# Input rows 20 KB apart in memory instead of 16 KB, in a kernel that multiplies pairs of fields

## The chip, the cores and the metric

The kernel runs on one core of one Trainium2 chip. The metric is the device time of one execution in microseconds (us). "Before" and "after" are the two kernels of the change. A run counts as slow when it is over 1.5% above the fastest of the same kernel, and as fast otherwise.

## The reference

```python
# x: (4096, 32, 64) float32, W: (64, 64) float32
vid = jnp.einsum('bfd,de->bfe', x, W)
idx_i, idx_j = jnp.triu_indices(32, k=1)          # 496 pairs of fields, i < j
return x[:, idx_i, :] * vid[:, idx_j, :]          # (4096, 496, 64)
```

The output has 520 MB and the input 33.6 MB, so this is mostly a matter of writing.

## The kernel before

The host lays x out as 16 tiles of 128 rows (two batch halves x 64 embedding elements). A row holds 32 fields of 128 samples, 512 B each, thus 16 KB; rows follow one another without a gap. One row goes to one SBUF partition. A tile is loaded in pieces of eight fields (the second tile in two of sixteen), so a piece is 128 runs of 4 KB, one from each row, and the distance from one run to the next is the row pitch.

```python
C = 128          # samples per row of a tile
SLOT = 83        # pairs per output buffer
# GROWING: sizes of the first 25 stores, so that stores start early and grow  [list cut]

    NT, _, F, _ = x.shape                    # 16 tiles, 32 fields
    xpool = ctx.enter_context(tc.tile_pool(name="x", bufs=2))
    opool = ctx.enter_context(tc.tile_pool(name="out", bufs=4))
    # [psum, const and scheduling cut]

    def load(t, pieces, queue):
        xt = xpool.tile([P, F, C], F32, tag="x", name=f"x_{t}")
        n = F // pieces
        for lo in range(0, F, n):
            queue.dma_start(out=xt[:, lo : lo + n, :], in_=x[t][:, lo : lo + n, :])
        return xt

    loaded = [load(0, 4, nc.sync), load(1, 2, nc.sync)]
    for t in range(NT):
        if 0 < t < NT - 1:
            loaded.append(load(t + 1, 4, nc.scalar))
        # TensorE: vid = W^T x for the tile, 8 PSUM banks            [cut]
        # VectorE: o[pair] = x[i] * vid[j], runs of i for one j      [cut]
        # SyncE: store each filled stretch of the output buffer      [cut]

# host
    x = x.reshape(2, NT, C, F, D).transpose(1, 0, 4, 3, 2).reshape(NT, 2 * D, F, C)
```

Of the kernel before, what the change touches and what calls it, by code (L numbers as in the profile page):

```python
# [1 line left out]

# [4 lines left out]

F32 = mybir.dt.float32
ALU = mybir.AluOpType

P = 128

C = 128

SLOT = 83

GROWING = [
    21, 24, 21, 17, 22, 15, 16, 30, 24, 20, 21, 18, 27, 24, 32, 46, 37, 50,
    31, 45, 38, 53, 30, 65, 18,
]  # L20


def first(j):

    return j * (j - 1) // 2


@with_exitstack
def pairwise_bilinear_kernel(
    ctx: ExitStack,  # L30
    tc: tile.TileContext,
    x: bass.AP,
    w: bass.AP,
    out: bass.AP,
):

    nc = tc.nc
    NT, _, F, _ = x.shape
    D = P // 2
    NP = F * (F - 1) // 2  # L40

    BANK = 512 // C


    ctx.enter_context(tc.manual_schedule(engines={mybir.EngineType.SP}))

    const = ctx.enter_context(tc.tile_pool(name="const", bufs=1))
    xpool = ctx.enter_context(tc.tile_pool(name="x", bufs=2))
    opool = ctx.enter_context(tc.tile_pool(name="out", bufs=4))
    psum = ctx.enter_context(  # L50
        tc.tile_pool(name="ps", bufs=8, space=bass.MemoryType.PSUM)
    )


    w2 = const.tile([P, D], F32)
    nc.sync.dma_start(out=w2, in_=w)  # L56
# [10 lines that stand above are left out]
    done = 0  # L67
    growing = iter(GROWING)
    until = next(growing)
# [3 lines that stand above are left out]
        xt = loaded[t]  # L73


        vid = []
        for b in range(0, F, BANK):
            pv = psum.tile([P, BANK, C], F32, tag="pv", name=f"pv_{t}_{b}")
            for h in range(2):
                half = slice(h * D, (h + 1) * D)  # L80
                nc.tensor.matmul(  # L81
                    pv[half, :, :],
                    lhsT=w2[half, :],
                    rhs=xt[half, b : b + BANK, :],
                    start=True,
                    stop=True,
                )
            vid.append(pv)

        sent = 0  # L90
        for j in range(1, F):
            i = 0
            while i < j:
                at = first(j) + i
                base = at - at % SLOT
                if at == base:
                    ot = opool.tile([P, SLOT, C], F32, tag="o", name=f"o_{t}_{at}")
                n = min(j - i, base + SLOT - at)
                nc.vector.tensor_tensor(  # L99
                    ot[:, at - base : at - base + n, :],  # L100
                    xt[:, i : i + n, :],
                    vid[j // BANK][:, j % BANK : j % BANK + 1, :].to_broadcast([P, n, C]),
                    ALU.mult,
                )
                i += n
                at += n
                if t * NP + at == until or at in (base + SLOT, NP):
                    nc.sync.dma_start(
                        out=out[t][:, sent:at, :],
                        in_=ot[:, sent - base : at - base, :],  # L110
                    )
                    sent = at
                    if t * NP + at == until:
                        until += next(growing, NT * NP)


_INS = ["r_x", "L0_rec_W"]
_OUTS = [((4096, 496, 64), "float32")]


# [32 lines left out]
```

## Time and profile before

| Before, profiled run | |
|---|---|
| median of three runs | 1294.66 us (1294.46 to 1294.67) |
| span in the profile | 1293.3 us |
| bytes moved, mean rate | 553.82 MB, 428 GB/s |
| VectorE busy | 1102.4 us (85%) |
| TensorE busy | 229.0 us (18%) |
| load packets of 4 KB in the steady state | 7168, median 159 ns |

A packet is one piece of a transfer as one DMA engine records it, here the run of one row.

The page cuts the span into 40 slices of 32 us: a digit is the busy share of a slice in tenths, and the row GB/s has what the 16 DMA engines moved in each. In the table of queues, q1 carries what SyncE issued (all stores and the first two tiles' loads) and q10 what ScalarE issued (the other loads), with packets, MB and the share of 16 engines' span. The chain of work that ended last is read backwards from the end; in its order of time each line is start, duration, and work. The lines themselves are in the prediction.

### The profile page before, as it was taken

Reading aid. Unit: us, or ns where it says so; the run is one execution under the profiler, and the core shown is the slowest. Engines: PE = TensorE matmul, PEld = TensorE weight load, DVE = VectorE, ACT = ScalarE, POOL = GpSimd, SP = SyncE. Lnnn points to the kernel's source line nnn. Section 1 sums busy time; section 2 is a strip of 40 time slices with the busy share of each in tenths; the row PEclk is TensorE's granted clock in tenths of the full one; section 3 lists DMA queues with packets and bytes.
Section 4 is the critical chain, followed back from the end, with each engine's and each line's share of the span. In section 5 each row is a group of like instructions: output and inputs, shape, how many; then the busy total and the mean of one; then the engine's idle time right before and its main releaser. Section 6 shows DMA issues by size and latency. Waiting matters only on the chain.

```text
span 1293.3 us, 2181 instructions
## 1 busy us (share of the span) xinstructions
PE 229.0 (18%) x512; PEld 49.5 (4%) x512; DVE 1102.4 (85%) x576; POOL 0.2 (0%) x4
## 2 busy tenths in 40 slices
PE   4121121211212112121121211203112031120000
PEld 1000000000000000000000000000000000000000
DVE  7999999888898888988888888888888888888970
POOL 0000000000000000000000000000000000000000
PEclk8555555555655555565555655556555565555555
DMA  9999999999999999999999999999999999999998
GB/s 376 427 410 434 434 433 434 431 433 431 434 431 433 431 432 433 432 431 435 432 431 433 432 435 426 437 427 433 434 430 435 430 431 436 428 436 431 438 431 348
DMA packets 25212, 553.82 MB, mean 428 GB/s; under 512 B 2928, under 2 KB 2928, under 8 KB 10736
## 3 DMA queue, kind: packets, MB, share of 16 engines
q1 hardware_dynamic: 17136, 524.33, 94.2%
q10 hardware_dynamic: 8064, 29.36, 5.6%
q8 instruction: 4, 0.07, 0.0%
q14 instruction: 8, 0.07, 0.0%
HBM read 33.59 MB, written 520.09 MB: 428 GB/s over the span
## 4 chain that ended last, share of the span: by engine, by line
DMA 66%; DVE 29%; issue 1%; DVEq 0%; PE 0%; SPq 0%
DMA out_dram<-o 65%; DVE o L99 29%; DMA x<-in_r_x_dram 0%; DVEq L145 0%; PE pv L81 0%; DVEq L99 0%; SPq L56 0%
## 5 line engine op out<-in xcount | busy, mean ns | idle before, releaser
L99 DVE TENSOR_TENSOR o<-x,pv 128x640 f32<-128x640 f32 (+14 forms) x576 | 1102.4, 1984 | 151.3 <-DMA out_dram<-o 142.2
L81 PE MATMUL pv<-x,w 64*64 64x512 f32 x512 | 229.0, 1027 | 951.7 <-DVE o L99 500.2
L81 PEld LDWEIGHTS pv<-x,w 64*64 64x64 f32 x512 | 49.5, 205 | 1129.5 <-issue 1124.8
L128 POOL MEMSET const-bfloat16-1.0<- 128x1 bf16 x1 | 0.1, 102 | 0.0
L128 POOL MEMSET const-uint8-127<- 128x1 uint8 x1 | 0.1, 102 | 0.0
L128 POOL MEMSET const-float32-0.0<- 128x1 f32 x1 | 0.1, 99 | 0.2 <-issue 0.2
L128 POOL MEMSET const-float32-1.0<- 128x1 f32 x1 | 0.1, 99 | 0.0
## 6 DMA issues: line engine op xcount, KB each, us to landing
out_dram<-o SPq DMA_DIRECT2D x72, 5312.0 KB, 41.4
out_dram<-o SPq DMA_DIRECT2D x15, 5184.0 KB, 42.3
x<-in_r_x_dram ACTq DMA_DIRECT2D x56, 512.0 KB, 31.9
out_dram<-o SPq DMA_DIRECT2D x3, 1536.0 KB, 8.3
out_dram<-o SPq DMA_DIRECT2D x1, 4160.0 KB, 23.5
out_dram<-o SPq DMA_DIRECT2D x3, 1344.0 KB, 6.4
out_dram<-o SPq DMA_DIRECT2D x2, 1920.0 KB, 15.3
out_dram<-o SPq DMA_DIRECT2D x1, 3392.0 KB, 22.2
```

What stands on the lines that cost most here:

```text
L81: nc.tensor.matmul(pv[half, :, :], lhsT=w2[half, :], rhs=xt[half, b : b + BANK, :], start=True, stop=True,)
L99: nc.vector.tensor_tensor(ot[:, at - base : at - base + n, :], xt[:, i : i + n, :], vid[j // BANK][:, j % BANK : j % BANK + 1, :].to_broad ...
L128: nc = _bacc.Bacc("TRN2", target_bir_lowering=False, num_devices=1, dynamic_dma_scratch_size=1024)
```

## The change

The change pads each row of x with eight unused fields, so that rows start 20 KB apart, which is not a power of two. Its hope is that reads from evenly spaced rows spread better over the memory. The pad is never loaded.

```diff
 SLOT = 83
+
+PAD = 8
...
-    NT, _, F, _ = x.shape
+    NT = x.shape[0]
+    F = x.shape[2] - PAD
...
     x = x.reshape(2, NT, C, F, D).transpose(1, 0, 4, 3, 2).reshape(NT, 2 * D, F, C)
+    x = _np.pad(x, ((0, 0), (0, 0), (0, PAD), (0, 0)))
```

## The prediction

> **What bounds the kernel now.** I read the page's table of busy time first, then its slices and queue table, then the chain of work that ended last, then the waits, and last the single packets of the two data queues.
>
> ```profile
> DVE  7999999888898888988888888888888888888970
> DMA  9999999999999999999999999999999999999998
> GB/s 376 427 410 434 434 433 434 431 433 431 434 431 433 431 432 433 432 431 435 432 431 433 432 435 426 437 427 433 434 430 435 430 431 436 428 436 431 438 431 348
> q1 hardware_dynamic: 17136, 524.33, 94.2%
> q10 hardware_dynamic: 8064, 29.36, 5.6%
> HBM read 33.59 MB, written 520.09 MB: 428 GB/s over the span
> DMA 66%; DVE 29%; issue 1%; DVEq 0%; PE 0%; SPq 0%
> ```
>
> The reader should see three things. The 16 DMA engines are at nine tenths or more in 39 of 40 slices, and from the fourth slice on they move 426 to 438 GB/s with no trend. The two queues together fill 94.2 + 5.6 = 99.8% of 16 engines' span, so there is no idle DMA time to speak of. And the traffic is lopsided: 520 MB are written, 34 MB read. VectorE is busy 1102.4 us of 1293.3 (85%), so it has 15% to spare.
>
> The chain in order of time shows how the bound works. Four output buffers circulate: VectorE refills one, its store queues behind three others, and when it lands the next refill may begin.
>
> ```profile
> 604.73 11.09 DVE o L99 x3
> ...
> 615.84 42.24 DMA out_dram<-o
> ...
> 658.17 11.49 DVE o L99 x5
> ```
>
> One lap is 11.1 + 42.2 = 53.3 us, four stores. A batch tile has six stores and one load, (496 + 32) x 64 KB = 34.6 MB; four sixths of it is 23.1 MB, and 23.1 MB in 53.3 us is 433 GB/s. So the lap is not a latency that some cleverness could shorten; it is the time in which the DMA engines move one lap's bytes. A store alone would need 5.44 MB / 433 GB/s = 12.6 us, and takes 41.4 us to land since it stands behind its predecessors.
>
> Last, the waits. They say whether a late load could hurt by its lateness alone.
>
> ```profile
> PE pv L81 <- DMA x<-in_r_x_dram: 432.0, 36, 16.9
> DVE o L99 <- DMA out_dram<-o: 142.2, 78, 3.2
> DVE o L99 <- PE pv L81: 9.1, 2, 8.4
> ```
>
> TensorE waits for the loads of x, but it is only 18% busy and runs ahead. VectorE waits for TensorE twice in the whole program, at the very start (8.4 us and the rest), and otherwise only for stores that free a buffer. Loads are therefore early enough; what they cost is the engine time that they take from the stores.
>
> **What the Trainium skill says.** The page "DMA: Bandwidth & Descriptors", section "Latency and other measured facts", is the one that bears on the change: with copies of 128 partitions it found 207 GB/s per direction at a row pitch of 512 KiB, 164 at 2 MiB, 103 at 4 MiB, and the full 214 when 4 KiB were added to the last. Its cause, channels hit in lock-step, it calls an inference. So padding does help where the pitch is a large power of two; but at 512 KiB the loss was already down to 3%, and here the pitch is 16 KiB, thirty-two times smaller. Whether this trace agrees is tested on the packets below. The same page, section "Where 436 GB/s comes from", gives a ceiling of 435.2 GB/s for one core's 16 engines. The trace agrees: a plateau of 433. The same page, section "Issuing engines are not separate DMA queues", says that transfers of all issuers share the same engines; q1 and q10 adding to 99.8% agree with it. So a microsecond of engine time saved or lost on loads is one saved or lost in the end.
>
> **The change part by part.** The code that runs is the same. Comparing the two builds, every engine has as many instructions in the same order (VectorE 576 multiplications, 62 loads of x, 112 stores); only line numbers move. The number of fields is taken from the padded shape less eight, so the pad is never loaded. Load pieces are still 4 KB per partition (two of them 8 KB, in the first two tiles' ramp), on-chip tiles keep their size, and the output's layout is untouched. Removed: nothing. Added on the device: nothing. Moved: the address at which each partition's row of x starts, 20 KB apart instead of 16, and with it, perhaps, where the allocator puts the tensors in memory, as x grows from 33.6 to 41.9 MB.
>
> So the only thing that can change is the time of a read packet. From the trace's packet records, leaving out those of a few bytes (mean of the loads, medians, ns):
>
> ```
> load  in the steady state   4096 B  x7168   median 159 (10th and 90th percentile both 159), mean 160.2
> load  at the start          4096 B  x512    median 159, 90th percentile 324, mean 200.4
> load  at the start          8192 B  x256 and stores of that size: median 309
> store                      42496 B  x9216   median 1571, mean 1573.0
> ```
>
> From the first and last row: (1571 - 159) / (42496 - 4096) = 0.03677 ns per byte, which is 27.2 GB/s for one engine and 435 for sixteen; the rest, 159 - 4096 x 0.03677 = 8.4 ns, is the same for a packet of 42 KB as for one of 4 KB. The 8 KB row lies on the same line: 8.4 + 301.2 = 309.6, measured 309. Reads at 16 KB pitch and writes at 248 KB pitch thus follow one law, and the reads scatter less than a nanosecond between the percentiles. A channel conflict would show as a longer or spread read packet; there is none to remove. That is my answer to whether the trace agrees with the skill: it does, in that at this small pitch nothing is lost.
>
> Sum of what the change can return:
> - Steady loads: 7168 packets x (159 - 159) = 0 us expected.
> - Scatter of the steady loads: 7168 x (160.2 - 159) / 16 engines = 0.5 us at the very most.
> - The start: 512 x (200.4 - 159) / 16 = 1.3 us of extra packet time. The 8 KB loads directly after it, at the same 16 KB pitch, run at the full rate, so I put this down to the start of an idle memory path and expect no more than a few tenths of it to change.
> - VectorE 1102.4 us, TensorE 229.0 us, stores 94.2%: no change.
>
> Expected: 1294.66 less about 0.2, say 1294.4 us.
>
> **The rivals.** *First: the 16 KB pitch does cost, and padding pays.* For it: it is a power of two, each 4 KB piece visits the same quarter of every 16 KB, and the mean rate of the load packets, 4096 / 160.2 = 25.6 GB/s per engine, is lower than the stores' 27.0. Against it: the 8.4 ns per packet explain that difference wholly. If even these vanished, 7168 x 8.4 / 16 = 3.8 us, plus the 1.3 us of the start, would give 1289.6 us, 0.4% faster. That is the ceiling of this rival; 2% (25.9 us) is out of reach, as all loads together hold only 71.8 us of the engines' time.
>
> *Second: the new pitch or the new places are worse.* Each 10% on a load packet is 7.2 us, and it would reach the end in full, as the DMA engines are the bound. To lose 2% a load packet would have to take 25.9 x 16 / 7168 = 58 ns more, 217 instead of 159. Against it: 20 KB is five times 4 KB and so less regular than 16, still a multiple of every alignment that the old rows had. The stores could be touched too if the output moved to other addresses: 0.2% on them is 2.4 us. That I hold possible and small; their rows of 248 KB pitch stay as they are.
>
> *Third: loads land later or earlier and shift buffers.* A piece takes 31.9 us to land because it shares engines with store packets ten times its size. A shift of a few us there is hidden: VectorE waits for no load after the start, and the order of store bytes does not alter their sum.
>
> **Range and chances.** The three runs of before lie within 0.2 us and the profiled one at 1295.1, so noise on one chip is under half a microsecond. I allow 3 us down (most of the first rival) and 3.5 us up (5% on load packets, or 0.2% on stores with a new place, or another chip): 1291.5 to 1298. Within 2%: 0.975. Faster by over 2% would need more than the loads can give: 0.01. Slower by over 2% needs 36% on each load packet, or a change to the stores that I do not see: 0.015.
>
> **What would show it.** In the profile after: q10 again 8064 packets, 29.36 MB and 5.6%; the steady load packet again 159 ns; q1 at 94.2%; a plateau of 433 GB/s and the lap of 53.3 us; VectorE at 1102 us. If padding pays, q10's share falls towards 5.3% and the load packet towards 151 ns; if it hurts, that share and the spread of its packets grow. A different mean at the start only, beside the same 159 ns later, would show that a pitch matters when reads run alone. The prediction is wrong if store packets change from 1571 ns, since that means that placement matters, which I counted as nearly nothing, or if packet counts change, since then the transfers were cut differently than the code suggests.

## The result

After: 1295.14 us median (1293.85 to 1296.49, four runs); before in the same rounds: 1294.66 us (1294.46 to 1295.46, four runs). The ratio is 1.0003, with a 95% interval of 0.9985 to 1.002. A ratio here is the mean time of one kernel's fast runs over that of the other's in the same rounds, so it is not quite the ratio of the quoted medians. Two later measurements of the same pair gave 1.0002 and 0.9983. The change is worth nothing that matters.

The page of the profile after, in the lines that answer to those of before:

```profile
DVE  7999999888887888888888888888888888888970
DMA  9999999999999999999999999999999999999997
GB/s 388 427 413 438 432 432 432 437 428 433 436 432 432 432 429 430 430 431 435 429 432 430 430 433 432 436 428 430 436 432 437 423 430 440 433 431 429 431 439 323
q1 hardware_dynamic: 17136, 524.33, 94.1%
q10 hardware_dynamic: 8064, 29.36, 5.6%
HBM read 33.59 MB, written 520.09 MB: 428 GB/s over the span
DMA 66%; DVE 29%; issue 2%; DVEq 0%; PE 0%; SPq 0%
```

Packets and bytes are equal to the last digit, the loads' share is 5.6% as before, and the plateau has not moved. The slices between differ by up to 8 GB/s either way; the first rose from 376 to 388 GB/s, the last fell from 348 to 323. Both are taken up below.

The lap of output buffers in the chain of after, at the place shown of before, and the waits:

```profile
605.73 11.10 DVE o L105 x3
...
616.84 42.33 DMA out_dram<-o
...
659.26 11.49 DVE o L105 x5
```

```profile
PE pv L87 <- DMA x<-in_r_x_dram: 429.9, 35, 17.0
DVE o L105 <- DMA out_dram<-o: 144.4, 79, 3.8
DVE o L105 <- PE pv L87: 8.2, 2, 7.5
```

One lap takes 53.4 us instead of 53.3. VectorE still waits for nothing but freed buffers after the start. Its first wait for TensorE, though, is 0.9 us shorter (8.2 instead of 9.1 in total). That is the one sign in these views that could be the new pitch's, and it sits at the start. The chain shows where it comes from, first of before, then of after (start, us, what):

```profile
1.17 5.12 DMA x<-in_r_x_dram
```

```profile
1.17 4.22 DMA x<-in_r_x_dram
```

The first load of 512 KB lands 0.9 us sooner. In stretches of 2 us the table of busy times by window shows the same; the last two columns are the DMA share and GB/s. Before, then after:

```profile
2.00:4.00 2.00, 0.00 (x0) 0.00 (x0) 0.00 (x0) 0.00 (x0) 1.00 0.82 184
4.00:6.00 2.00, 0.00 (x0) 0.00 (x0) 0.00 (x0) 0.00 (x0) 1.00 0.94 309
6.00:8.00 2.00, 1.58 (x4) 0.59 (x6) 0.00 (x0) 0.00 (x0) 1.00 1.01 371
```

```profile
2.00:4.00 2.00, 0.00 (x0) 0.00 (x0) 0.00 (x0) 0.00 (x0) 1.00 0.75 201
4.00:6.00 2.00, 0.48 (x2) 0.32 (x4) 0.00 (x0) 0.00 (x0) 1.00 1.02 416
6.00:8.00 2.00, 2.00 (x6) 0.52 (x4) 0.47 (x2) 0.00 (x0) 1.00 1.04 426
```

From 4 to 6 us the reads run at 416 GB/s instead of 309. Whether that is the pitch or luck, and whether it reaches the end, one profile cannot say.

### The profile page after: what moved, and what is told of

It reads as the page before. It is cut to its first block, busy times and chain, and to the rows that moved or that the text cites. A ratio compares the mean times of both kernels' runs of the same rounds, so it can differ in the third digit from the quotient of the medians.

```text
span 1294.7 us, 2181 instructions
## 1 busy us (share of the span) xinstructions
PE 230.7 (18%) x512; PEld 49.5 (4%) x512; DVE 1102.6 (85%) x576; POOL 0.2 (0%) x4
## 4 chain that ended last, share of the span: by engine, by line
DMA 66%; DVE 29%; issue 2%; DVEq 0%; PE 0%; SPq 0%
DMA out_dram<-o 65%; DVE o L105 29%; DMA x<-in_r_x_dram 0%; DVEq L152 0%; PE pv L87 0%; DVEq L105 0%; SPq L62 0%
```

## The experiments

**Theory:** in the steady state the pitch of 16 KB costs nothing, so padding returns nothing there. **Rival one:** it does cost when reads run alone, which would show at the start or in a phase of reads. **Rival two:** what moves is the placing of tensors, not the pitch. **A doubt about the method:** perhaps this kernel would not show a bad pitch at all.

### Noise, and the start again: both kernels unchanged, five rounds

> The kernel before, unchanged, against itself: it gives the noise. Theory (the pitch does nothing): 1294.7 us within 2 us, ratio 1.000 with an interval about as wide as that of the change (0.9985 to 1.002), steady load packets at 159 ns. For the start: if the slower first load packets (mean 200 ns in the profile before) belong to the 16 KB pitch, they come again at 195 to 205 ns; if they belong to the run, the mean falls anywhere between 165 and 210.

> The changed kernel again. Theory: 1294 to 1296 us, ratio to before between 0.999 and 1.001, steady load packets 159 ns. Rival (a small real gain or loss of the pitch under the noise): a ratio that stays clear of 1 with the same sign as in the first measurement, 1.0003. For the start: if the pitch sets it, the first 512 load packets have a mean near 176 ns again; if the run sets it, the mean is spread like that of the kernel before.

Before against itself: 1295.18 us, ratio 1.0002 (0.999 to 1.0015). After: 1295.32 us, ratio 1.0002 (0.9989 to 1.0014). The two differ from before by as much as before does from itself. Steady load packets have means of 160.1 and 159.8 ns and a median of 159. The first 512 load packets came out at 207.0 ns for before and 184.2 for after, the first landing at 5.24 and 4.06 us. The slow start of the 16 KB rows therefore belongs to the kernel and not to the run.

### Reads alone: all of x read once more ahead of everything

```diff
+    for t in range(NT):
+        bt = opool.tile([P, SLOT, C], F32, tag="o", name=f"b_{t}")
+        for lo in range(0, F, 8):
+            nc.sync.dma_start(out=bt[:, lo : lo + 8, :], in_=x[t][:, lo : lo + 8, :])
     loaded = [load(0, 4, nc.sync), load(1, 2, nc.sync)]
```

> Before, with all of x read once more ahead of everything in 64 pieces of 512 KB into the output buffers (results unchanged): reads alone, 8192 packets of 4 KB at the 16 KB pitch. Theory: packets of 159 ns as in the steady state, 33.5 MB at 435 GB/s, so 77 us more plus a start of 2 to 4 us, 1372 to 1380 us. Rival (the 16 KB pitch costs when reads run alone): packets at 176 to 200 ns, 9 to 21 us more than in the same kernel with 20 KB rows.

> The same reads ahead in the changed kernel, at the 20 KB pitch. Theory: the same time as with the 16 KB rows within 2 us, packets at 159 ns. Rival: 9 to 21 us less than with the 16 KB rows, with packets at 159 ns here and longer there.

The times are 1377.41 us (16 KB) and 1378.78 us (20 KB): the padded kernel is, if anything, the slower one. The chains of reads, 16 KB first, then 20 KB:

```profile
3.05 8.34 DMA b<-in_r_x_dram
...
11.41 10.22 DMA b<-in_r_x_dram
```

```profile
3.04 7.24 DMA b<-in_r_x_dram
...
10.30 10.22 DMA b<-in_r_x_dram
```

The first piece of the chain is 1.1 us longer with 16 KB rows; every later one of these extra reads is 10.22 us in both kernels. In the middle of the phase the windows (last column GB/s) agree as well, 16 KB first:

```profile
40.00:50.00 10.00, 0.00 (x0) 0.00 (x0) 0.00 (x0) 0.00 (x0) 1.00 1.03 410
```

```profile
40.00:50.00 10.00, 0.00 (x0) 0.00 (x0) 0.00 (x0) 0.00 (x0) 1.00 1.03 410
```

Rival one falls for sustained reads: with nothing but reads on the engines, both pitches give 410 GB/s. The cost of the 16 KB pitch is paid once, in the first ten microseconds. My expectation used 435 GB/s and forgot the fixed part of each packet; with packets of 161 ns (the median of the phase) 8192 x 161 / 16 = 82.4 us, and the measured difference of the means is 1377.48 - 1295.14 = 82.3. That the padded kernel was 1.3 us slower here although its first piece landed 1.1 us sooner is taken up with the last slice, below.

### Placement alone: 16 KB rows in a tensor of the padded size

```diff
-    NT, _, F, _ = x.shape
+    NT = out.shape[0]
+    F = x.shape[2]
...
+    x = _np.pad(x, ((0, NT // 4), (0, 0), (0, 0), (0, 0)))
```

> Rows of x stay 16 KB apart, but the tensor is as large as after the change (four unused tiles at its end), so that only the placing of tensors in memory can differ. Theory: 1293.5 to 1296.5 us, load packets 159 ns, store packets 1571. Rival (placement moves the stores): store packets off 1571 by over 0.2%, over 2 us.

Measured: 1294.94 us, ratio 0.9991 (0.9974 to 1.0008). Large store packets have a mean of 1573.7 ns (before: 1573.0). The start is the slow one: first landing 5.13 us, first packets 203.0 ns. So the size of the tensor does not make the start quick. The trace has no addresses, so that the output really moved is not shown.

### Much larger pitches: 256 KB, 4 MB, and 4 MB + 4 KB

The host lays x out by partition, so that one row holds all 16 tiles; ROWS and EXTRA set the pitch, (16 x ROWS + EXTRA) x 512 B.

```diff
+ROWS = 32      # 512 for 4 MB
+EXTRA = 0      # 8 for the 4 KB
...
-            queue.dma_start(out=xt[:, lo : lo + n, :], in_=x[t][:, lo : lo + n, :])
+            queue.dma_start(out=xt[:, lo : lo + n, :], in_=x[:, t * ROWS + lo : t * ROWS + lo + n, :])
...
-    x = x.reshape(2, NT, C, F, D).transpose(1, 0, 4, 3, 2).reshape(NT, 2 * D, F, C)
+    x = x.reshape(2, NT, C, F, D).transpose(0, 4, 1, 3, 2).reshape(2 * D, NT, F, C)
+    x = _np.pad(x, ((0, 0), (0, 0), (0, ROWS - F), (0, 0))).reshape(2 * D, NT * ROWS, C)
+    x = _np.pad(x, ((0, 0), (0, EXTRA), (0, 0)))
```

> x laid out by partition, so that the 128 rows of one load lie 256 KB apart, no padding. Theory (at pitches of this size nothing aliases): load packets 159 to 163 ns, 1294 to 1297 us. Rival (any large power of two costs something): packets at 175 ns or more, 1302 us or more.

> The same with rows 4 MB apart. A check that the pitch of the loads can be seen at all in this kernel and that engine time of loads reaches the end in full. Theory: the Trainium skill found half the rate at 4 MiB, so load packets near 320 ns, 7168 x 161 / 16 = 72 us more and up to 5 us at the start: 1360 to 1375 us. Rival (the slow reads hide beside the stores, or store packets of 1.6 us between them leave the memory time to recover): packets under 200 ns, under 1315 us.

(The figure of the Trainium skill is that of the page and section that the prediction names.)

> Rows 4 MB and 4 KB apart: the padding of the change applied where the pitch is bad. Theory: full rate again, packets 159 ns, 1294 to 1297 us. Rival (the cost at 4 MB comes from the spread of the reads over much memory, not from the power of two): as slow as with 4 MB.

At 256 KB: 1294.06 us, ratio 0.9986 (0.9971 to 1.0001), steady load packets 160.3 ns. At 4 MB: 1390.99 us, ratio 1.0736 (1.0718 to 1.0754). At 4 MB + 4 KB: 1293.74 us, ratio 0.9982 (0.9967 to 0.9996). So a bad pitch exists and this kernel shows it; 4 KB of padding removes it wholly; and 16 KB is not one in the steady state.

The profile at 4 MB is worth reading, since it differs from what I expected: load packets near 320 ns and 1360 to 1375 us were forecast, and they took 188.8 ns on average with 1391 us in all. The theory was off in both; its rival had the packets right and the time wrong (first the page's slices and queues, then the first load in the chain, then the windows while it waits and one of the steady state):

```profile
GB/s 156 429 375 331 431 386 412 408 387 426 388 416 401 402 416 402 413 397 401 416 392 421 398 400 414 392 422 392 404 408 389 428 387 407 407 395 433 435 433 358
q1 hardware_dynamic: 17136, 524.33, 92.6%
q10 hardware_dynamic: 8064, 29.36, 6.1%
```

```profile
1.16 14.44 DMA x<-in_r_x_dram
```

```profile
2.00:4.00 2.00, 0.00 (x0) 0.00 (x0) 0.00 (x0) 0.00 (x0) 1.00 0.17 65
4.00:6.00 2.00, 0.00 (x0) 0.00 (x0) 0.00 (x0) 0.00 (x0) 1.00 0.12 49
6.00:8.00 2.00, 0.00 (x0) 0.00 (x0) 0.00 (x0) 0.00 (x0) 1.00 0.15 57
```

```profile
600.00:700.00 100.00, 15.16 (x34) 3.50 (x36) 80.47 (x46) 0.00 (x0) 0.53 1.00 403
```

The last window again, of before and of after, for comparison:

```profile
600.00:700.00 100.00, 16.84 (x38) 3.49 (x36) 85.82 (x47) 0.00 (x0) 0.52 1.01 434
```

```profile
600.00:700.00 100.00, 18.22 (x40) 3.49 (x36) 85.64 (x45) 0.00 (x0) 0.55 1.00 431
```

Summing the trace's packet records over 16 engines, 4 MB against before:

```
steady loads, 4 KB                  +12.8 us   (mean 160.2 -> 188.8 ns, median 159 in both)
large stores, 42 KB and 41 KB       +60.1 us   (mean of the 42 KB ones 1573.0 -> 1651.2 ns)
everything else                     +11.5 us
all packets                         +84.5 us   (1291.0 -> 1375.5)
span                                +99.1 us   (1293.3 -> 1392.4), so 14.6 us are gaps, 12.4 of them in the first 20 us
```

Only an eighth of the loss stands in the steady load packets. In the first microseconds, with nothing but loads under way, the engines show a share of 0.12 to 0.17, and the load packets there average 169 ns: the waiting is outside the packet records. In the steady state it is the stores beside the loads whose records grow. In the packet records of the 4 MB run, 4048 of the 42 KB stores have no load packet starting during them or within 0.4 us of them, on any engine, and took 1571 ns on average; the other 5168 took 1714 (before: 1572 and 1574). In the window from 600 to 700 us the engines look as full as ever (DMA share 1.00) and move 403 GB/s. That is why the rate on the plateau, and not the load packet alone, has to be looked at. By that measure 16 KB and 20 KB are alike (434 and 431 in this window, 433 and 432 GB/s from 300 to 1100 us).

### What makes the start slow at 16 KB: 32 KB, 16.5 KB, and two kernels once more

The edits are one number: PAD = 32 and PAD = 1 in the kernel after.

> 32 unused fields, rows 32 KB apart, a power of two again. What makes the start slow at 16 KB? If powers of two do, the first load lands after 5 us or more. If rows close together do (the start was 5.1 us at 16 KB, 4.1 at 20 KB, 3.5 at 256 KB), it lands after 3.6 to 4.0 us. In both cases 1293 to 1296.5 us and steady load packets of 159 ns.

> One unused field, rows 16.5 KB apart. If powers of two make the start slow, the first load lands after 4.0 to 4.3 us as with 20 KB; if rows close together do, after 4.9 to 5.2 us. In both cases 1293 to 1297 us and steady load packets of 159 ns.

> The changed kernel once more, for its start. In three profiles with 16 KB rows the first load landed 5.1 to 5.2 us after its issue, in two with 20 KB rows after 4.1 and 4.2. Theory (the pitch sets the cold start, about 1 us, and this 1 us of DMA time is returned at the end but drowns in noise of 1 to 2 us): first landing at 4.0 to 4.3 us, 1293.5 to 1296 us, ratio 0.998 to 1.000. Rival (the end takes it back or the noise holds no gain): the same start and a ratio of 1.000 to 1.001.

> Rows 4 MB and 4 KB apart again; its first measurement gave 0.9982 of the time before. Theory (its faster start, 3.7 us instead of 5.1, is worth 1.5 us in the end): 0.9985 to 0.9992, first landing at 3.5 to 3.8 us. Rival (chance): 0.9995 to 1.001.

All profiles of the normal kernels together, by pitch:

| rows apart | profiles | first load lands after, us | first 512 load packets, mean ns | steady load packets, mean ns |
|---|---|---|---|---|
| 16 KB (before, before again, larger tensor) | 3 | 5.12, 5.24, 5.13 | 200, 207, 203 | 160.2, 160.1, 160.6 |
| 16.5 KB | 1 | 3.60 | 179 | 160.4 |
| 20 KB (after, three times) | 3 | 4.22, 4.06, 3.86 | 176, 184, 179 | 160.0, 159.8, 160.0 |
| 32 KB | 1 | 3.80 | 183 | 160.8 |
| 256 KB | 1 | 3.45 | 180 | 160.3 |
| 4 MB + 4 KB (twice) | 2 | 3.65, 3.64 | 172, 176 | 160.5, 160.5 |
| 4 MB | 1 | 14.44 | 169 | 188.8 |

Both of my explanations of the slow start fall. Powers of two as such are not it, since 32 KB and 256 KB start quickly. Closeness of the rows is not it, since 16.5 KB starts quickly. Of the small pitches tried, exactly 16 KB is slow, and the cause stays open. Where the table has one profile, it is one observation. With 20 KB rows the third landing, 3.86 us, was below the 4.0 to 4.3 expected.

Times of these four kernels, measured together: 20 KB 1294.77 us, ratio 0.9983 (0.9971 to 0.9995); 4 MB + 4 KB 1295.0 us, 0.9988 (0.9975 to 1.0001); 32 KB 1294.85 us, 0.9989 (0.9972 to 1.0005); 16.5 KB 1294.54 us, 0.9984 (0.997 to 0.9998). These look like gains, but across the sets of runs it was before that moved: its mean beside them was 1296.89 us, against 1294.81, 1295.14 and 1295.94 in the three sets of runs ahead (the last three sets ran on three different chips). After stayed at 1295.15, 1295.29 and 1294.82. That the start's 1 us, 0.08%, is returned at the end fits the interval of each of the three measurements of after; that nothing is returned fits the first two. The times leave it open.

The traces say somewhat more. The sum of all packets over 16 engines is 1291.03, 1291.01 and 1291.52 us in the three profiles with 16 KB rows and 1290.70, 1290.40 and 1290.59 with 20 KB rows, 0.6 us less on average. What can hide it is the last slice, which comes in two sizes whatever the pitch: 342 to 351 GB/s in six of the table's eleven profiles without the one at 4 MB, with spans of 1292.1 to 1293.4 us, and 323 to 329 in five, with spans of 1294.1 to 1294.9. The profile of after fell in the second kind, that of before in the first. Among the first kind, 16 KB rows give 1293.3 and 1293.4 and all others 1292.1 to 1292.2; among the second, 16 KB gives 1294.9 and the others 1294.1 to 1294.7. I sorted them so after seeing them, and one side has only three profiles, so this suggests a gain of about 1 us and does not prove it. The packet records show what the two sizes are: 8 us before the end all 16 engines still move data in the six profiles of the first kind, but only 6 to 8 packets are under way in the five of the second. Idle engine time in the last 20 us is then 6.7 to 7.4 us instead of 5.1 to 5.8 (mean over 16 engines). The reads-alone pair shows the same: with 20 KB rows the packets sum to 0.9 us less, but the engines idle for 9.2 us of the last 20 instead of 6.1, and the span is 2.1 us longer. So the engines do not finish together, and how unevenly they do outweighs the start. Why is not known.

No version beats both kernels by an amount that these runs resolve: rows 4 MB + 4 KB apart had means of 1293.70 and 1295.24 us in their two sets of runs, and after lies between 1294.8 and 1295.3.

## Why the prediction was right, point by point

- **The bound.** Right. The DMA engines are full, the plateau is 433 and 432 GB/s, and the lap of four stores is 53.3 and 53.4 us. That extra engine time reaches the end was shown by the reads ahead: with 84.0 and 83.4 us more in packets (16 and 20 KB rows) the spans grew by 82.1 and 82.9. The expected time, 1294.4 us, is 0.7 below the measured median, which is within the noise. One reading of the lines was loose: the rate is 426 to 438 GB/s only up to the slice before the last, which has 348.
- **Steady loads return nothing.** Right: 159 ns median before and after, 410 GB/s at both pitches when reads run alone. The prediction drew its law through loads and stores together, where a fixed cost of the reads would have passed for one of every packet. Stores alone settle it: 7680 B in 291 ns and 42496 B in 1571 (medians) give 159.2 ns for 4096 B, and the loads took 159. Its "all loads together", 71.8 us, are the steady ones alone; with those of the start it is 83 us, so its ceiling for rival one holds for the steady loads plus the start's excess.
- **The start.** This is the term that was mis-sized. The prediction counted 1.3 us of extra packet time there, put it down to "the start of an idle memory path", and expected "no more than a few tenths" to change. In three against three profiles 16 KB rows average 203.5 ns in the first 512 load packets and 20 KB rows 179.7: 512 x 23.8 / 16 = 0.8 us, more than half of the 1.3, and the first load lands 1.1 us sooner. The argument that 8 KB loads at the same pitch ran at full rate failed because they came later: in the phase of reads alone, 4 KB pieces at 16 KB pitch were just as fast once the first ten microseconds had passed. The prediction's sign "that a pitch matters when reads run alone" came true at the start only, and the run of reads alone shows that it did not mean what was said. Rival one was thus right about the start, within the ceiling that the prediction gave it; through what mechanism is open.
- **The noise.** "Under half a microsecond" was too small: unchanged kernels spread from 1294.3 to 1296.9 in one set of runs, and before itself from 1294.9 to 1298.9 in another. The range held since it allowed for other things that did not come.
- **The placement rival.** Store packets stayed within 0.1% (mean 1572.6 to 1573.8 ns for those of 42 KB) in every kernel with a good pitch. Nothing of it was seen; that the output moved in memory is not shown.
- **The price of a bad pitch.** The prediction measured it on the load packet ("each 10% is 7.2 us"). The 4 MB run shows that this sees too little: steady load packets grew by 12.8 us in all, with a 90th percentile of 260 ns, while the span grew by 99. "A channel conflict would show as a longer or spread read packet" was thus true of the smaller part only. The conclusion for 20 KB stands, as stores and plateau were unchanged too, but as a test the load packet was incomplete.
- **The Trainium skill.** "DMA: Bandwidth & Descriptors", section "Latency and other measured facts", holds in direction: 4 MB is bad, 4 KB of padding restores it (1293.74 us against 1390.99). It was right to read its small loss at 512 KiB as a sign that 16 KB would lose nothing steady. The section "Where 436 GB/s comes from" gave a ceiling of 435.2 GB/s; from 300 to 1100 us before ran at 433 and after at 432. The same section has a second limit, about 358 GB/s on the memory's side, which the prediction passed over; with one core at work it did not hold here.

## What to carry to other kernels

Before padding an input, look at how much of the bounding resource it uses: here the steady loads held 5.6% of the DMA engines' time and all loads 6.4%, and 4 KB reads already ran at the rate that their size allows, so the layout could not return more than a few microseconds. If a pitch is suspected, compare the plateau in GB/s and the packets of the neighbouring stores, not only the packets of the loads. For a start that sets no more than 1 us, measure the first landing in several profiles; whole times with a noise of 1 to 2 us will not show it.

## What the Trainium skill lacked or had wrong

- "DMA: Bandwidth & Descriptors", section "Latency and other measured facts": its row on large row pitches starts at 512 KiB. Here pitches of 16, 16.5, 20, 32 and 256 KB all gave steady load packets of 160 to 161 ns on average, and padding was worth nothing in the steady state.
- The same row has no word on the first microseconds. With 16 KB rows the first 512 KB load landed after 5.1 to 5.2 us, with 16.5 KB to 256 KB after 3.5 to 4.2, and with 4 MB after 14.4.
- The same row gives about half the rate at 4 MiB (for copies within HBM). Reads of 4 KB alone ran far lower here in the one stretch that shows them, the start: 49 to 65 GB/s between 2 and 8 us, against 184 to 371 at 16 KB; beside stores the total fell only from 433 to 405 GB/s.
- No page read for this case says where a slow read shows in a trace: at 4 MB, of 84.5 us more packet time only 12.8 stood in the steady loads, and 60.1 in the large stores beside them.
- "DMA: Bandwidth & Descriptors" has no measured time of a packet against its size for transfers issued from SyncE or ScalarE on this chip; its fit of time against bytes is for the GpSimd path. Here a load or store packet took 8.4 ns + 0.0368 ns per byte, which made reads alone in 4 KB packets run at 410 GB/s and stores of 42 KB at 433.
